# Routing groups of one and three batches in layer 0, norms batch by batch, and the next attention's first scores between the last up and down projections

## The chip, the cores and the metric

The kernel runs on one core of a Trainium2 chip. The metric is device time of one launch in microseconds. Three runs of the kernel before took 1347.03, 1354.06 and 1354.34 us; their median is 1354.06.

The engines are named as the profile names them: PE (TensorE: matmuls and transposes), DVE (VectorE), ACT (ScalarE), POOL (GpSimd) and SP (SyncE, which issues most of the transfers). Each engine executes one sequence of instructions; semaphores order them against each other.

## What is computed

Four layers, each an attention from 4 x 512 tokens (128 features) to 154 context tokens per batch, and then a mixture of 8 experts:

```python
x = x + L0_attention(layernorm(x), ctx)              # similarity features @ W_qv
x = x + L0_experts(layernorm(x))                     # top 2, (x W0 + b0) * silu(x W1 + b1), hidden 512
x = x + L1_attention(ctx, ctx, layernorm(x), mask)   # 16 heads of 8
x = x + L1_experts(layernorm(x))                     # top 1 with a capacity, gelu, hidden 512
x = x + L2_attention(layernorm(x), ctx)              # 16 heads of 64, its own norm, gated by tanh
x = x + L2_experts(layernorm(x))                     # top 2, gelu, hidden 256
x = x + L3_attention(layernorm(x), ctx, ctx)         # 16 heads of 64
x = x + L3_experts(layernorm(x))                     # top 2, relu, hidden 512
```

Layer 0's attention, for one batch:

```python
Sim  = (hc @ w1)[:, :, None] + (hq @ w2)[:, None, :] + einsum("bid,bjd->bij", hc * w3, hq) + b
A    = softmax(Sim, axis=2);  hq_hat = A @ hq
Batt = softmax(max(Sim, axis=2), axis=1);  hc_bar = Batt @ hc
out  = concat([hc, hq_hat, hc * hq_hat, hc * hc_bar]) @ W_qv + b_qv
```

The experts' part of the reference computes every expert for every token and weights the results; only the chosen one or two of each token count.

## The kernel before

**Tiles.** The tokens of a batch are four tiles of 128 rows (`NI` = 4), kept on chip as `x[b]` for the whole kernel. Attention works on one tile of a batch at a time in layers 1 to 3, and on a whole batch in layer 0.

**Routing.** The experts of a layer are computed in two halves, of batches 0 and 1 and of batches 2 and 3. `route` (L651) works on one half in steps with yields between: statistics, norm of both batches (L659), transposes (L251 in a helper), logits by the gate matrix, the best one or two experts (`top`), ranks of the tokens within their expert by matmuls with triangular and full matrices of ones (L693, L695), and from them a slot for each chosen pair of token and expert. The slots lie in blocks of 128, each block belonging to one expert. An indirect transfer on POOL (`scatter`, L721 and L722) writes 128 rows of the normed tokens to a DRAM buffer `buf[half]`; a half needs 16 of them with two choices and 8 with one. `BLK` gives the number of blocks, 23 with two choices (16 full ones at most, and 7 partly filled) or 15 with one.

**Experts.** `experts` (L825) is a generator too. SP loads tokens in groups of four blocks (`load`), which waits for all scatters of the half; PE transposes them (`tokens`, L850). For each block (or two, `PER`) `up` (L855) reads the expert's number, SP loads its weights, 516 KB in layer 0, into one of three buffers, and PE multiplies (L877); `down` (L882) of the block before applies the activation, multiplies by `w2` (L916), which holds all experts' down weights, copies the result on DVE and stores it to `ybuf[half]`. So a down always follows the next block's up.

**Gathering back.** `gather` (L948) queues indirect loads on POOL (L953) which bring each token's rows back; `row_transfers` (L641) takes the next `n` of the queued row transfers, scatters and gathers alike, and ties each to an instruction beside which it is to start. `combine` (L965) adds a token tile's gathered rows, weighted, to `x` (L971, DVE). A gather waits for all stores of the half; a `combine` of the first half was written behind the issue of all the half's gathers.

**Order.** `Steps` wraps a generator so that the main loop can interleave it with others by hand. The main loop (L1356 on) for a layer: the attention, with the combines of the last layer's second half and the routing of this layer's first half stepped beside it; the first experts, with the second half's routing; then the second experts, with the first half's gathers and combines and the preparation of the next attention (`at.early`: keys, values or masks; `at.late`: norm, transposes, queries). In the attentions of layers 2 and 3 PE, ACT and DVE keep the order as written (`wide_period`), in that of layer 1 PE and ACT do (`narrow_period`); elsewhere, layer 0's attention among it, a scheduler chooses each engine's order from its own estimate of times. Layer 0's attention (`attend_first`, L1278) prepares batches 0 to 3 (similarity and exponentials) and then finishes each in `tile_of` (L1026): transposes of the probabilities (L1033, L1038), their product with the context (L1041, L1042), the maxima over the tokens (L1048, L1051), `hcp` (L1060) and the output product.

Of the kernel before, what the change touches and what calls it, by code (L numbers as in the profile page):

```python
# [19 lines left out]
P = 128  # L20
# [6 lines left out]
E = 8  # L27
H = 16
CAP = int(B * S / E * 1.25) + 1
NH = NT // 2  # L30
EPS = 1e-5
NEG = -1e20
BLK = (2 * NH + E - 1, NH + E - 1)
UPS = (2, 1, 1, 1)
NF = (4, 4, 2, 4)
PER = (1, 2, 2, 2)


# [9 lines left out]
def tile_xattn_moe_stack(ctx: ExitStack, tc: tile.TileContext, a: dict, out: bass.AP):  # L48
# [101 lines left out]
    for base, sign in ((0, 1), (D // H - 1, -1)):  # L150
# [17 lines left out]
    fill = const.tile([P, E, NH], F32, name="fill")  # L168
    nc.gpsimd.iota(
        fill, pattern=[[0, E], [P, NH]], base=0, channel_multiplier=0, allow_small_or_imprecise_dtypes=True  # L170
# [6 lines left out]
    nth = const.tile([1, BLK[0], E], F32, name="nth")  # L177
    nc.gpsimd.iota(
        nth, pattern=[[1, BLK[0]], [0, E]], base=0, channel_multiplier=0, allow_small_or_imprecise_dtypes=True
# [59 lines left out]
    def norm(src, found, pool=None):  # L239
        mv, rstd = found  # L240
        xn = (pool or xnp).tile([P, NI, D], F32, tag="xn", name="xn", bufs=3 if pool else 2)
        for i in range(NI):
            nc.vector.tensor_scalar(
                xn[:, i, :], src[:, i, :], mv[:, i, 0:1], rstd[:, i : i + 1], ALU.subtract, ALU.mult
            )
        return xn
# [23 lines left out]
    class Tile:  # L270
# [31 lines left out]
        def exp(self, g):  # L302
            if g == 0:
                self.pr = p2.tile([P, H, S2], F32, tag="probs", name="probs")
            for s in range(min(3, 8 - 3 * g)):
                for j in range(2):
                    h = self.at.heads(None, 3 * g + s, j)
                    nc.scalar.activation(  # L308
# [5 lines left out]
                    )  # L314

# [44 lines left out]
        def take_ends(self, engine):  # L360
            self.tails = p2.tile([self.rows, 4, P], F32, tag="tails", name="tails")
# [124 lines left out]
    def wide_period(new, old, nxt=None, middle=nothing, queries=nothing, parts=nothing, after=nothing, older=None):  # L486

        if new:
            new.score(0)
# [3 lines left out]
        if new:  # L493
            new.most(0)
# [41 lines left out]
    def attention64(b, gather_x, wq, wk, wv, wo, add):  # L536
# [36 lines left out]
        def values_ends():  # L573
# [3 lines left out]
            for r in range(2):  # L577
                rows = slice(64 * r, 64 * r + 64)
                nc.tensor.matmul(q[rows, :], ct2[:, b], wv[:, r * 512 : (r + 1) * 512], start=True, stop=True)
# [6 lines left out]
            at.vt = at.vt.rearrange("p c s d -> p (c s d)")  # L586

# [35 lines left out]
    def rsm(name, *shape, dt=F32):  # L623
        return rt.tile([P, *shape], dt, tag=name, name=name)

    def top(lg):

        m = rt.tile([P, NH], F32, tag="m", name="m", bufs=4)
        nc.vector.tensor_reduce(m, lg, AX.X, ALU.max)
        eq = rt.tile([P, NH, E], F32, tag="eq", name="eq", bufs=4)  # L630
        nc.vector.tensor_tensor(eq, lg, bc(m, 2, E), ALU.is_equal)
        nc.vector.tensor_tensor(eq, eq, bc(rev_e, 1, NH), ALU.mult)
        r = rt.tile([P, NH], F32, tag="r", name="r", bufs=4)
        nc.vector.tensor_reduce(r, eq, AX.X, ALU.max)
        oh = rt.tile([P, NH, E], F32, tag="oh", name="oh", bufs=4)
# [5 lines left out]
    def row_transfers(n=2 * NH, behind=None):  # L641
# [9 lines left out]
    def route(layer, half, wg, bg, b2):  # L651

        lg = rsm("lg", NH, E)
        found = [stats(x[2 * half + k]) for k in range(B // 2)]
        yield
        xns = [norm(x[2 * half + k], found[k], rt) for k in range(B // 2)]  # L659
        yield  # L660
        xnTs = [transposed(xn) for xn in xns]
        yield
        for k, xnT in enumerate(xnTs):
            q = ps_tr()
            for i in range(NI):
                nc.tensor.matmul(q[:, i * E : (i + 1) * E], xnT[:, i * P : (i + 1) * P], wg, start=True, stop=True)
            o = lg[:, k * NI : (k + 1) * NI, :]
            qv = q[:, 0 : NI * E].rearrange("p (i e) -> p i e", i=NI)
            if bg is None:
                nc.vector.tensor_copy(o, qv)  # L670
            else:
                nc.vector.tensor_tensor(o, qv, bc(bg, 1, NI), ALU.add)
        yield
# [3 lines left out]
        sel = rsm("sel", NH + 1, E, dt=BF16)  # L677
        nc.vector.memset(sel[:, NH, :], 0.0)
        if layer == 1:
            nc.vector.tensor_copy(sel[:, 0:NH, :], oh1)  # L680
        else:
            yield
            lg2 = rsm("lg2", NH, E)
# [3 lines left out]
            nc.vector.tensor_tensor(sel[:, 0:NH, :], oh1, oh2, ALU.add)  # L687
# [3 lines left out]
        n = (NH + 1) * E  # L691
        q = ps_tr()
        nc.tensor.matmul(q[:, 0:n], before, sf, start=True, stop=False)  # L693
        for s in range(1, NH + 1):
            nc.tensor.matmul(q[:, s * E : n], ones_b, sf[:, 0 : n - s * E], start=False, stop=(s == NH))  # L695
# [737 lines left out]
```

## Time and profile before

| Quantity | Value |
|---|---|
| Median of three runs | 1354.06 us |
| The profiled execution | 1282.47 us |
| Its span | 1280.8 us |
| Mean granted PE clock | 0.917 of full speed |
| First expert matmul of layer 0 | 108.3 us |
| Layer 0's experts, 46 blocks | 108.3 to 260.5 us |
| Layer 1's attention | 259 to about 499 us |
| Layer 1's experts, to the end of the stage | about 481 to 574 us |
| Layer 2's attention | 571 to 817 us |
| Layer 3's attention | 904 to 1152 us |
| Last PE work | about 1251 us |

The profile is of one execution, and its times below are counted from the start of the span. The profiled execution was shorter than the median of the timed runs, so a difference read in the profile is to be set against 1282.47 us and then scaled.

Two rows of groups give the indirect transfers, of 128 rows each, which POOL issues (columns: line, engine, operation, what is written from what, count; busy time in all, mean ns of one; idle time of the engine just before, and what ended most of it):

```profile
L953 POOL DMA_INDIRECT yg<-ybuf,su x112 | 106.7, 952 | 246.5 <-ACT pT L267 59.9
L722 POOL DMA_INDIRECT buf<-xn,su x112 | 109.6, 979 | 227.0 <-DVE eb L745 97.3
```

### The profile page before, as it was taken

To read this page: it belongs to the slowest core of one execution; us is meant where nothing else is said; L and a number is where in the kernel's file an instruction comes from. 1 tells how busy PE (TensorE), PEld (TensorE's weight loads), DVE (VectorE), ACT (ScalarE), POOL (GpSimd) and SP (SyncE) were. 2 spreads that over 40 slices of the span, in tenths; PEclk is the share of its full clock that TensorE was granted. 3 is DMA by queue.
4 is the path that set the end of the run, shared out by engine and by line. 5 is a ranking of instruction groups with operands and counts; after the bars stand their busy time and mean duration, and the time that the engine had idled before them with its cause. 6 is when DMAs were issued, how large, how long until landed. Compare 5 with 4: busy or idle time off the path is not lost.

```text
span 1280.8 us, 26318 instructions
## 1 busy us (share of the span) xinstructions
PE 1089.4 (85%) x9351; PEld 896.9 (70%) x9351; DVE 731.6 (57%) x2012; ACT 565.3 (44%) x2264; POOL 253.6 (20%) x281
## 2 busy tenths in 40 slices
PE   4787998977878888889999998966899999899990
PEld 3657998933435448787878777855778788789890
DVE  6554646567666763335665776424476576646352
ACT  2113433454554543546656565321656665532230
POOL 2041315023000010232000004045220000402334
PEclk8767999988898988998999999887999999999996
DMA  7023786721100314433112214444421111334762
GB/s 228 1 81 113 216 253 189 207 94 25 23 19 26 100 38 119 133 110 84 35 35 55 64 37 123 123 150 133 127 55 45 41 35 35 109 95 143 209 191 60
DMA packets 136064, 126.77 MB, mean 99 GB/s; under 512 B 12538, under 2 KB 115583, under 8 KB 135551
## 3 DMA queue, kind: packets, MB, share of 16 engines
q1 hardware_dynamic: 128767, 110.39, 30.5%
q0 software_dynamic: 7168, 14.69, 3.9%
q8 instruction: 77, 1.26, 0.4%
q14 instruction: 52, 0.43, 0.1%
HBM read 101.31 MB, written 23.72 MB: 98 GB/s over the span
## 4 chain that ended last, share of the span: by engine, by line
PE 59%; DVE 12%; DMA 9%; issue 8%; ACT 5%; POOL 5%; SPq 2%; POOLq 0%; DVEq 0%
PE sc L877 11%; PE av L916 6%; PE tr L371 6%; PE sc L607 5%; PE av L408 5%; PE tr L425 5%; PE sc L592 3%; DMA yg<-ybuf,su 3%; POOL yg L953 3%; ACT probs L308 3%; DVE nm L294 3%; PE sc L1175 2%; DMA w<-in_up 2%; PE av L390 2%; PE tr L358 2%
## 5 line engine op out<-in xcount | busy, mean ns | idle before, releaser
L308 ACT ACTIVATE probs<-sc,nm 128x154 f32<-128x154 f32 x768 | 286.9, 403 | 162.7 <-DVE nm L294 162.5
L877 PE MATMUL sc<-tokT,w 128*128 128x128 f32 x1528 | 201.3, 286 | 8.7 <-DMA w<-in_up 3.6
L877 PEld LDWEIGHTS sc<-tokT,w 128*128 128x128 f32 x1528 | 189.0, 200 | 15.5 <-ACT eg L900 5.2
L294 DVE TENSOR_REDUCE nm<-sc 128x6 f32<-128x924 f32 x144 | 142.6, 1007 | 74.8 <-PE sc L607 49.1
L308 ACT ACTIVATION_READ_ACCUMULATOR probs<-sc,nm 128x1 f32 x768 | 168.3, 219 | 0.0
L916 PE MATMUL av<-w,hT 128*128 x1160 | 155.3, 279 | 3.2 <-DVE hT L905 2.5
L953 POOL DMA_INDIRECT yg<-ybuf,su x112 | 106.7, 952 | 246.5 <-ACT pT L267 59.9
L722 POOL DMA_INDIRECT buf<-xn,su x112 | 109.6, 979 | 227.0 <-DVE eb L745 97.3
L916 PEld LDWEIGHTS av<-w,hT 128*128 128x128 f32 x1160 | 141.9, 193 | 8.9 <-issue 4.7
L236 POOL TENSOR_TENSOR rstd<-ve,nhalf 128x4 f32<-128x4 f32 x32 | 33.0, 1032 | 547.3 <-DVE ve L234 429.6
L264 DVE COPY pT<-tr 128x512 f32<-128x512 f32 x160 | 106.9, 684 | 45.3 <-PE tr L371 41.5
L408 PE MATMUL av<-pT,vm 128*64 128x128 f32 (+1 forms) x1536 | 106.2, 284 | 22.5 <-DVE pT L264 22.4
L371 PE MATMUL tr<-ident,probs 128*128 128x128 f32 x768 | 123.1, 291 | 1.5 <-DVE rT L337 1.5
L371 PEld LDWEIGHTS tr<-ident,probs 128*128 128x128 f32 x768 | 86.1, 146 | 33.4 <-issue 21.7
L408 PEld LDWEIGHTS av<-pT,vm 128*64 128x64 f32 (+1 forms) x1536 | 63.8, 126 | 55.7 <-DVE pT L264 30.9
L900 ACT ACTIVATE eg<-sc,w 128x128 f32<-128x128 f32 x184 | 52.9, 368 | 89.5 <-PE sc L877 82.1
L607 PE MATMUL sc<-kT,qT 64*128 64x154 f32 x1024 | 87.1, 308 | 4.8 <-ACT probs L308 4.8
L905 DVE SCALAR_TENSOR_TENSOR hT<-sc,w,eg 128x128 f32<-128x128 f32 x184 | 56.2, 342 | 51.0 <-ACT eg L900 51.0
L607 PEld LDWEIGHTS sc<-kT,qT 64*128 64x128 f32 x1024 | 71.3, 189 | 15.8 <-issue 9.9
L592 PE MATMUL sc<-xnT,wq 128*128 128x128 f32 x512 | 73.6, 303 | 4.7 <-ACT probs L308 2.3
L592 PEld LDWEIGHTS sc<-xnT,wq 128*128 128x128 f32 x512 | 67.3, 212 | 10.2 <-issue 3.6
L425 PE MATMUL tr<-wo,aT 128*128 128x128 f32 x512 | 66.2, 284 | 1.6 <-DVE xnT L256 1.3
(255 smaller groups left out, 1432.2 us busy)
## 6 DMA issues: line engine op xcount, KB each, us to landing
w<-in_up SPq DMA_DIRECT2D x46, 516.0 KB
w<-in_up SPq DMA_DIRECT2D x76, 258.0 KB
rep<-rd SPq DMA_DIRECT2D x64, 256.0 KB
tok<-buf SPq DMA_DIRECT2D x36, 256.0 KB
ybuf<-ys SPq DMA_DIRECT2D x58, 128.0 KB
w<-in_down SPq DMA_DIRECT2D x3, 2048.0 KB
w<-in_up SPq DMA_DIRECT2D x46, 128.0 KB
ybuf<-ys SPq DMA_DIRECT2D x52, 64.0 KB
```

The source lines that it names most:

```text
L264: return nc.vector.tensor_copy(o, i)
L294: nc.vector.tensor_reduce(self.at.heads(self.nm, g, n), self.sc[g][:, :, 0 : n * S2].rearrange("p j (s k) -> p j s k", s=n), AX.X, ALU.max ...
L308: nc.scalar.activation(self.pr[:, h, :], self.sc[g][:, j, s * S2 : (s + 1) * S2], AF.Exp, bias=self.nm[:, h : h + 1], accum_out=self.rs[:, ...
L371: nc.tensor.transpose(q[:, t * P : (t + 1) * P], self.pr[:, h, 0:P], ident)
L408: nc.tensor.matmul(av[rows, cols], v, self.pT[n][:, t, :], start=False, stop=last)
L425: nc.tensor.matmul(o[:, 0:D], self.aT[:, c, :], self.at.wo[:, c, :], start=(c == 0), stop=(c == self.nb - 1))
L592: nc.tensor.matmul(sc[:, c // 4, c % 4 * P : (c % 4 + 1) * P], wq[:, c * P : (c + 1) * P], at.xnT[:, i * P : (i + 1) * P], start=True, sto ...
L607: nc.tensor.matmul(sc[:, j, s * S2 : (s + 1) * S2], at.qT[i][rows, c, :], at.kT[rows, c, :], start=True, stop=True)
L722: ins = nc.gpsimd.indirect_dma_start(out=buf[half], out_offset=bass.IndirectOffsetOnAxis(ap=su[:, t : t + 1], axis=0), in_=xns[t // NI][:, ...
L877: nc.tensor.matmul(dst, w[:, b, at : at + P], xT, start=True, stop=True)
L916: nc.tensor.matmul(y[:, b * D : (b + 1) * D], hT[:, fc, :], w2[:, bass.ds(es[b], 1), fc, :].rearrange("p o d -> p (o d)"), start=(fc == 0) ...
L953: ins = nc.gpsimd.indirect_dma_start(out=yg[:, t, :], out_offset=None, in_=ybuf[half], in_offset=bass.IndirectOffsetOnAxis(ap=su[:, t : t ...
```

## The change

- **Groups.** The halves become groups of batches by layer, `GROUPS`: in layer 0 the first group is batch 0 alone and the second is batches 1 to 3; in the other layers they stay as they were. Layer 0 then has 15 blocks in the first group and 31 in the second. Tiles, buffers and loops follow (`nt` in place of `NH`).
- **Single norms.** In layer 0, and for the second group everywhere, `route` takes statistics, norm, transposes and logits one batch at a time. The second group's route begins within the attention: in layer 0 beside `attend_first`, in the others after tile 1 of batch 3.
- **Layer 0's attention** gets its PE order as written; `tile_of` becomes a generator with a yield in its middle, and the product with the context moves behind the transpose of the maxima.
- **Gathers** are kept for each batch apart (`Gathered`). The first group's first `NI * TOP` gathers are issued at once, others with the downs (2 + n each instead of 2 n) or, for a `combine` that needs them, just ahead of it.
- **Layer 1.** Its setup moves behind the first experts of layer 0; its parts for each next batch are distributed over the tiles anew; and the exponentials of its first tile release three row transfers for each group of heads.
- **Token transposes** of the second group stand behind the early parts of the next attention (`ahead`).
- **First scores.** After the last block's up projections, and before its down projections, the next attention's first group of scores and its maximum are written; the first period then leaves them out.
- **Buffers.** Several routing tiles and `tails` get one buffer in place of two or four, the normed tiles of the routing four in place of three, and `yg` six of half the size in place of two.

```diff
+GROUPS = (((0,), (1, 2, 3)), ((0, 1), (2, 3)), ((0, 1), (2, 3)), ((0, 1), (2, 3)))
+TOP = (2, 1, 2, 2)
+def most_blocks(layer, half):
+    return TOP[layer] * NI * len(GROUPS[layer][half]) + E - 1
...
-        found = [stats(x[2 * half + k]) for k in range(B // 2)]
-        yield
-        xns = [norm(x[2 * half + k], found[k], rt) for k in range(B // 2)]
-        yield
-        xnTs = [transposed(xn) for xn in xns]
-        yield
+        for some in ([b] for b in batches) if layer == 0 or half else (batches,):
+            found = [stats(x[b]) for b in some]
+            if layer:
+                yield
+            new = [norm(x[b], f, rt) for b, f in zip(some, found)]
+            if layer:
+                yield
+            xnTs = [transposed(xn) for xn in new]
...
             for c in range(m):
-                nc.tensor.transpose(q[:, c * P : (c + 1) * P], tok[:, c, :], ident)
+                ins = nc.tensor.transpose(q[:, c * P : (c + 1) * P], tok[:, c, :], ident)
+                if g == 0:
+                    wait_for(ins, ahead, "they fill the wait for the tokens")
...
-                2 * n, nc.vector.tensor_copy(ys[:, 0:n], y[:, 0 : n * D].rearrange("p (b d) -> p b d", b=n))
+                2 + n, nc.vector.tensor_copy(ys[:, 0:n], y[:, 0 : n * D].rearrange("p (b d) -> p b d", b=n))
...
+        while got[k].begun < NI * len(routed[1]):
+            row_transfers(1)
+        for (cw, _), yg in zip(routed[1], got[k].rows):
+            nc.vector.scalar_tensor_tensor(xi, yg[:, i, :], cw[:, t : t + 1], xi, ALU.mult, ALU.add)
...
+        first, second = (Steps(route(layer, half, *gates[layer])) for half in range(2))
+        with tc.manual_schedule(engines={mybir.EngineType.PE}):
+            tiles = [prepare(b, found[b]) for b in range(2)]
+            tiles[0].step()
+            tiles[0].finish()
+            tiles.append(prepare(2, found[2]))
+            tiles[1].step()
+            first.step()
+            tiles[1].finish()
+            first.step(2)
+            tiles.append(prepare(3, found[3]))
+            first.step()
+            tiles[2].step()
+            first.step()
+            second.step()
+            tiles[2].finish()
+            first.step(2)
+            tiles[3].step()
+            second.step()
+            tiles[3].finish()
+            first.finish()
+        return first.result, second
...
+                    elif b == 3 and i == 1:
+                        first = beside.finish()
+                        beside = Steps(route(layer, 1, *gates[layer]))
...
-            at.parts = ((masks,), (xn, values), (xnT,), (keys_queries,))
+            at.parts = ((masks,), (values,), (xn,), (xnT, keys_queries))
...
-        second = Steps(route(layer, 1, *gates[layer]))
+        if layer:
+            second.step(4)
+            first.step(2 // PER[layer])
         while not second.done:
             second.step(2)
             first.step(2 // PER[layer])
         routed.append(second.result)
         stores = first.finish()
         row_transfers()
-        got = gather(0, routed[0], stores)
+        got = gather(layer, 0, routed[0], stores)
+        row_transfers(NI * TOP[layer])
+        early = ()
         if layer < 3:
+            if layer == 0:
+                prepare = setups[1]()
             at = prepare(0, found)
-            for part in at.early:
-                part()
-        second = Steps(experts(layer, 1, routed[1], w2)).step((9, 3, 5, 5)[layer])
+            early = [part() for part in at.early][-1:]
+        second = Steps(experts(layer, 1, routed[1], w2, early)).step((3, 2, 2, 2)[layer])
...
             at.queries(0)
+            second.step(-(-most_blocks(layer, 1) // PER[layer]) - second.taken)
+            at.tile = Tile(at, 0)
+            at.tile.score(0)
+            at.tile.most(0)
         stores = second.finish()
```

## The prediction

> **What bounds the kernel now.** I read the page's sums first. TensorE (PE) is busy 85% of the span and heads the chain that ended last, but that share is a mean over stages, so the row of 40 slices of 32 us, in tenths, says where it is not full.
>
> ```profile
> span 1280.8 us, 26318 instructions
> PE 1089.4 (85%) x9351; PEld 896.9 (70%) x9351; DVE 731.6 (57%) x2012; ACT 565.3 (44%) x2264; POOL 253.6 (20%) x281
> PE   4787998977878888889999998966899999899990
> PE 59%; DVE 12%; DMA 9%; issue 8%; ACT 5%; POOL 5%; SPq 2%; POOLq 0%; DVEq 0%
> ```
>
> The low digits stand at slices 0 to 3 (layer 0's attention), 8 to 10 (start of layer 1's attention), 26 and 27 (layer 2 to layer 3) and the end. The first and third are what the change can reach most directly; there I asked what PE waited for (columns: instruction, releaser, us in total, times, longest). From 0 to 110 us, then from 800 to 920 us:
>
> ```profile
> PE tr L251 <- DVE xn L243: 7.9, 2, 4.4
> PE tr L850 <- DMA tok<-buf: 6.5, 1, 6.5
> ...
> PE tr L693 <- DVE sel L687: 5.5, 1, 5.5
> ```
> ```profile
> PE tr L850 <- DMA tok<-buf: 11.0, 2, 10.1
> PE tr L251 <- DVE xn L243: 11.0, 2, 10.2
> ```
>
> L850 is the first transpose of an expert stage: it waits until the last scattered row has landed and the token block is read back. The timeline (start, length, instruction, in brackets the idle time before it and its releaser) shows why the routing blocks layer 0's attention: batch 2's `sim` is ready at 47 us, its transposes run at 69, because PE's sequence has the rank matmuls of the first half (L693) ahead of them.
>
> ```profile
> 47.01 0.79 DVE L1029 TENSOR_TENSOR sim<-sim,srinv 128x616 f32<-128x616 f32 x1
> ...
> 68.67 0.24 PE L693 MATMUL tr<-sel,before 128*128 128x72 bf16 x1 [5.48 <-DVE sel L687]
> ...
> 69.03 1.09 PE L1033 MATMUL tr<-ident,sim 128*128 128x128 f32 x4
> ```
>
> Between layers 2 and 3, 16 scatters fill POOL, PE waits for tokens, then the gathers come late and the next norm is late with them:
>
> ```profile
> 834.85 1.02 POOL L722 DMA_INDIRECT buf<-xn,su  x1 [14.98 <-DVE eb L745]
> ...
> 854.07 0.96 POOL L722 DMA_INDIRECT buf<-xn,su  x1 [0.30 <-issue]
> ...
> 859.38 1.97 PE L850 MATMUL tr<-ident,tok 128*128 128x128 f32 x8 [10.14 <-DMA tok<-buf]
> ...
> 867.16 0.98 POOL L953 DMA_INDIRECT yg<-ybuf,su  x1 [12.12 <-DVE ys L925]
> ```
>
> **What the skill says.** The Trainium skill, "TensorE: Matmul & The Clock Gate", section "Part 1: The HAM clock gate (the 'warmup' mystery)": PE's clock drops after an idle stretch and needs some us of work to return. The trace agrees: 0.62 granted in 64 to 96 us and 0.76 in 864 to 896, against 0.97 over layer 0's experts. The same page, section "The mechanism": matmuls start and end in program order, so one that waits holds all behind it; the L693/L1033 lines agree. "DMA: Bandwidth & Descriptors", section "Anatomy of one DMA — SWDGE (gpsimd) path": about 2 us fixed per transfer, mostly the confirmation. Here scatters land 2.3 us after issue and gathers 2.3 to 3.8, while POOL issues one every 1.27 us (0.96 and 0.30 idle), so for a series the pace decides. Same page, section "Issuing engines are not separate DMA queues": all transfers share the 16 engines; agrees, as layer 0's last `ybuf` store takes 7.12 us behind the 2 MB `in_down` load.
>
> **The change part by part**, summed against the profiled execution (1282.5 us, span 1280.8).
>
> *Layer 0, start of the experts.* They start at 108.3 us. After, the first group is batch 0 alone: 8 scatters (8 x 1.27 = 10 us) in place of 16, issued during later batches. The written order keeps the rank matmuls off the other batches' path. The three waits named above sum to 7.9 + 6.5 + 5.5 = 20 us; some of the norm's waits are early loads and stay. Worked the other way: layer 0's attention runs from about 12 to 98 us, some 64 of them with PE busy at a mean clock of 0.71; four batches at about 15.7 us each in an undisturbed rhythm, plus a tail, end at 88 to 91. I take a start at 90: **-18** (-14 to -24).
>
> *Layer 0, between the groups.* This is the price. The first group lasts 15 blocks, not 23. A block takes 152.2 / 46 = 3.3 us with its side work, so it ends at 90 + 50 = 140. The second group needs batch 3, then the ranks (over 12 tiles), slots and 24 scatters. Before, the second half's first scatter was issued at 140.15, 32 us after its experts began, behind both batches' norms; with batches 1 and 2 already done I take 28 us: 118.5. Then 24 x 1.27 = 30.5 gives 149; landing 2.3, the token read behind the weights on SP, some 3: 155. PE idles from 140 to 155, less some 2 us of layer 1's early keys and values, which the change puts ahead of the token transposes: **+13** (0 to +18). SP's queue also holds the next weight loads behind the token read; these 516 KB loads came at about 200 GB/s, 2.5 us each, inside the upper bound. The trace shows no token wait between 108 and 260 before, so this wait is new.
>
> *Layer 0, side work.* Batch 2's norm, transposes and logits leave the experts for the attention, about 3 us of PE at most: **-3**. Total blocks are 46 both times, hence no change in expert work. Moving layer 1's setup behind the first experts' start is paid nowhere: the ups cover it, in bounds ±1. Together layer 0 gives **-8** (0 to -18).
>
> *Layer 1's attention.* Before, 16 second-half gathers run from 274 to 300 us; VectorE's combines wait for them, 59 us in 58 waits over the run, and tile 3 of that stretch takes 20.8 us against 11 to 14 of its neighbours. After, there are 24 rows: 8 x 1.27 = 10 us more on POOL, three batches' worth of combines spread over more periods. VectorE runs in order, so a late combine holds the copies behind it (`pT`, for which PE waits). The exps release three rows each early on, which hides most: **+3** (0 to +9; up to +25 in the rival below).
>
> *Layer 1 to 2.* Gathers of the first batch go first, single norms spread the second route: **-2** (-4 to +2).
>
> *Layer 2 to 3.* The first batch's 8 gathers stand right behind the scatters, and its combine waits for these alone. `xn` was there at 888.8; 8 gathers from about 858 (8 x 1.27, landing 3) and the combines and norm give 871 to 874. The 10.2 us wait shrinks to about 3: **-7** (-5 to -11). The token wait of 10.1 stays, since its 16 scatters stay and only the second route is begun earlier; were it to vanish, a further -8.
>
> *Layer 3's second half* has earlier combines: **-1**. The end does not move: from 1251 us on PE is idle, 16 gathers and the last stores remain.
>
> *Scores and maximum between the last up and down projections.* The kernel before already runs them there, since the scheduler placed them so:
>
> ```profile
> 571.47 0.80 PE L607 MATMUL sc<-kT,qT 64*128 64x154 f32 x8
> 572.19 0.94 PE L916 MATMUL av<-w,hT 128*128 x6
> 573.06 0.53 PE L607 MATMUL sc<-kT,qT 64*128 64x154 f32 x2
> 573.93 1.31 PE L607 MATMUL sc<-kT,qT 64*128 64x154 f32 x14
> 574.50 2.15 DVE L294 TENSOR_REDUCE nm<-sc 128x6 f32<-128x924 f32 x2 [0.17 <-PE sc L607]
> ```
>
> Two of three score groups lie around the downs; what is left is one maximum of about 1 us per start: **-1** (0 to -3 over three layers).
>
> *Buffers* falling from 4 or 2 to 1 (`eq`, `t5`, `tails` and the like) are free while their users are in order on VectorE; `tails` (pt) with one buffer couples neighbouring batches: 0 to +3, taken as 0.
>
> Sum: -8 + 3 - 2 - 7 - 1 - 1 = **-16** us. The median of the runs, 1354.06, is 1354.06 / 1282.5 = 1.056 of the profiled execution; scaled, -17: **1337 us**. About 1% (13.5 us) is what can be told from no change.
>
> **Rivals.**
> *Given back in layer 0 and 1.* The second group's tokens come after 165 us instead of 155, since 24 scatters in a row cannot begin earlier; the wait then passes 18 us and with it goes the whole gain of layer 0, leaving -7 - 1 - 2 + 3, some -7 or less: 1347 (1341 to 1360). For it: scatters before began 32 us after the experts. Against: two of three batches are routed before. Chance 0.28.
> *Slower.* At layer 1's start the rows behind the first nine are issued only as the combines ask for them. VectorE is in order, so each pair costs a landing, about 3.5 us, before the next pair can be asked for: 6 or 7 such pairs on the copies' path make +20 to +26 in place of +3. If layer 0 gives less than 10 us, the sum is over zero: 1366 (1360 to 1378). For it: 59 us of combine waits are there already. Against: the exps issue rows ahead. It decides once tile periods beside the gathers pass 20 us for more than one tile. Chance 0.17.
> *Larger gain.* The second group's early route hides its wait, the 10.1 us before layer 3 go as well: -35 to -45, 1313 (1300 to 1322). Chance 0.12.
> *The named part does nothing* is what I assume already; it changes the attribution, 1 us, not the time.
>
> **The numbers.** Main case (1322 to 1346, at 1337) 0.43. Faster by over 1%, below 1340.5: 0.12 + about 0.37 of the main case + 0.03 = 0.52; slower: 0.17 + 0.01 = 0.18; within 1%: 0.30. The range 1308 to 1366 leaves out the lower end of the large gain and the upper half of the slower case.
>
> **What would show it.** Right: first expert matmul near 90; a new token wait at L850's successor around 140 to 155; xn wait before layer 3 about 3 us; downs at the same places. Wrong: layer 0's attention not shorter than 86 us, no token wait between the groups, or tile periods over 20 us in layer 1.

## The result and the profile after

The changed kernel is slower by 1.2%: median 1364.31 us (1358.43 to 1371.0, 9 runs) against 1347.70 (1341.67 to 1354.34, 9 runs) for the kernel before, ratio 1.0118 [1.0085, 1.0152]. (A ratio is a kernel's time over that of the kernel before, measured beside it, with its 95% interval.) The forecast was 1337 us, with a range of 1308 to 1366 and a chance of 0.18 for slower by over 1%.

The runs were made on several chips, and the kernel before takes about 1278 us on chip 4 and 1344 to 1350 us on chips 0, 7 and 8, so times are compared only with runs of the kernel before on the same chip. For the first trace of the kernel before (1282.47 us) and for the trace of the changed kernel (1368.49) no chip is on record, but the first agrees with chip 4 and the second with the others; their difference of 86 us is not what the change costs, and the factor of 1.056 by which the forecast scaled its sum is one between chips. The page of the changed kernel, with the rows shown of before:

```profile
span 1366.8 us, 26291 instructions
PE 1117.8 (82%) x9351; PEld 914.1 (67%) x9351; DVE 732.2 (54%) x2012; ACT 563.9 (41%) x2264; POOL 253.6 (19%) x281
PE   5779599957778788988999987948889999798881
PE 58%; DVE 14%; issue 8%; DMA 6%; ACT 5%; another core or an unknown queue 3%; POOL 3%; SPq 2%; POOLq 0%; DVEq 0%; ACTq 0%
```

PE, VectorE, ScalarE and POOL execute as many instructions as before. A slice is 34 us here. The low digits are where they were, with a new one at slice 4 (137 to 171 us), between layer 0's groups of experts, and a lower one at slice 8, the start of layer 1's attention. PE's waits there, from 135 to 180 us and from 268 to 330 us:

```profile
PE av L945 <- DVE hT L934: 6.7, 2, 6.4
PE tr L877 <- DMA tok<-buf: 4.4, 1, 4.4
PE sc L906 <- DVE tokT L98: 3.4, 1, 3.4
PE sc L906 <- issue: 2.4, 5, 1.2
```
```profile
PE av L419 <- DVE pT L273: 12.5, 3, 5.2
PE tr L382 <- DVE rT L348: 7.1, 1, 7.1
PE tr L369 <- DVE res L1234: 4.0, 2, 3.2
```

The first is the forecast wait between the groups, 17 us in four pieces. In the trace of `no_named` (below; 130 to 180 us), from chip 4, it is a single wait for the tokens:

```profile
PE tr L875 <- DMA tok<-buf: 12.0, 1, 12.0
```

The second is VectorE's: copies that PE needs come late. In the kernel before (`before_again`, 261 to 325 us) the same two waits were:

```profile
PE av L408 <- DVE pT L264: 6.7, 4, 2.9
PE tr L371 <- DVE rT L337: 0.8, 1, 0.8
```

The new first scores stand where the change puts them (timeline of the changed kernel: last up, the downs with the scores in between):

```profile
606.20 1.06 PE L906 MATMUL sc<-tokT,w 128*128 128x128 f32 x8
607.10 1.95 PE L945 MATMUL av<-w,hT 128*128 x16
608.98 1.06 PE L621 MATMUL sc<-kT,qT 64*128 64x154 f32 x12
609.96 1.16 PE L945 MATMUL av<-w,hT 128*128 x8
```

Four traces come from chip 4 and can be set side by side. `no_named` is the changed kernel without the first scores; it takes the same time as the changed one (below). Stages in us, from starts and ends in the timelines ("up" and "down" are an expert's two projections; `late_route` and `no_exp_rows` are experiments below, each the changed kernel with one part taken back):

| Stage | before, again | no_named | late_route | no_exp_rows |
|---|---|---|---|---|
| start to layer 0's first up | 109.0 | 96.2 | 98.3 | 98.5 |
| layer 0's experts, to the last down | 152.6 | 157.6 | 160.1 | 160.6 |
| layer 1's attention, to the next up | 220.6 | 235.4 | 233.9 | 220.4 |
| layer 1's experts | 95.6 | 99.4 | 91.7 | 94.7 |
| layer 2's attention | 232.4 | 231.8 | 229.1 | 230.1 |
| layer 2's experts | 98.9 | 92.0 | 90.5 | 90.1 |
| layer 3's attention | 236.0 | 237.2 | 236.4 | 237.2 |
| layer 3's experts | 106.8 | 111.6 | 110.2 | 110.8 |
| from the last down to the end | 28.5 | 28.3 | 28.7 | 28.2 |
| span | 1280.4 | 1289.7 | 1278.9 | 1270.7 |

Layer 0's start gains, though less than forecast, and layer 2's experts gain as forecast. Layer 1's attention takes 15 us more, layer 1's and layer 3's experts 4 and 5. A stage that no edit touches differs by up to 5 us between these traces (layer 0's last down: 253.9, 258.5, 259.1), so one difference of this size is not read by itself, only where several runs repeat it. The spans of the first two columns differ by 9 us, the medians of their timed runs by 15 (1278.35 and 1293.59): the table doesn't place all of the loss.

A *period* below is the time from the reciprocal of one attention tile (`rinv` on VectorE) to that of the next tile.

### The profile page after: what moved, and what is told of

It is laid out like the page before. It is cut to its first block, busy times and chain, and to the rows that moved or that the text cites. A ratio compares the mean times of both kernels' runs of the same rounds, so it can differ in the third digit from the quotient of the medians.

```text
span 1366.8 us, 26291 instructions
## 1 busy us (share of the span) xinstructions
PE 1117.8 (82%) x9351; PEld 914.1 (67%) x9351; DVE 732.2 (54%) x2012; ACT 563.9 (41%) x2264; POOL 253.6 (19%) x281
## 4 chain that ended last, share of the span: by engine, by line
PE 58%; DVE 14%; issue 8%; DMA 6%; ACT 5%; another core or an unknown queue 3%; POOL 3%; SPq 2%; POOLq 0%; DVEq 0%; ACTq 0%
PE sc L906 11%; PE av L945 8%; PE tr L382 6%; PE av L419 5%; PE sc L621 5%; PE tr L436 4%; ACT probs L317 2%; PE sc L1220 2%; DVE nm L303 2%; PE sc L606 2%; PE av L401 2%; POOL yg L990 2%; PE tr L369 2%; DVE pT L273 1%
## 5 line engine op out<-in xcount | busy, mean ns | idle before, releaser
L906 PE MATMUL sc<-tokT,w 128*128 128x128 f32 x1528 | 210.9, 290 | 27.8 <-issue 19.1
L906 PEld LDWEIGHTS sc<-tokT,w 128*128 128x128 f32 x1528 | 195.0, 204 | 36.2 <-issue 27.4
L945 PE MATMUL av<-w,hT 128*128 x1160 | 160.9, 287 | 26.3 <-ACT hT L915 10.6
L945 PEld LDWEIGHTS av<-w,hT 128*128 128x128 f32 x1160 | 147.3, 200 | 34.6 <-issue 13.1
L382 PE MATMUL tr<-ident,probs 128*128 128x128 f32 x768 | 124.4, 294 | 7.9 <-DVE rT L348 7.9
L382 PEld LDWEIGHTS tr<-ident,probs 128*128 128x128 f32 x768 | 87.4, 147 | 39.8 <-issue 23.0
L954 DVE COPY ys<-av 128x256 f32<-128x256 f32 (+1 forms) x110 | 39.1, 357 | 85.7 <-PE av L945 57.0
L436 PE MATMUL tr<-wo,aT 128*128 128x128 f32 x512 | 72.2, 301 | 2.6 <-DVE xnT L265 1.3
L436 PEld LDWEIGHTS tr<-wo,aT 128*128 128x128 f32 x512 | 68.2, 214 | 4.7 <-DVE xnT L265 1.9
```

What stands on the lines that cost most here:

```text
L382: nc.tensor.transpose(q[:, t * P : (t + 1) * P], self.pr[:, h, 0:P], ident)
L436: nc.tensor.matmul(o[:, 0:D], self.aT[:, c, :], self.at.wo[:, c, :], start=(c == 0), stop=(c == self.nb - 1))
L906: nc.tensor.matmul(dst, w[:, b, at : at + P], xT, start=True, stop=True)
L945: nc.tensor.matmul(y[:, b * D : (b + 1) * D], hT[:, fc, :], w2[:, bass.ds(es[b], 1), fc, :].rearrange("p o d -> p (o d)"), start=(fc == 0) ...
```

## The experiments

**The kernel before, again.**

> The kernel before, unchanged, to have a profiled execution that lies near its timed ones: the first one's span was 1281 us where nine timed runs lay between 1342 and 1354. If that execution was an exception, this span is near 1347 and some stages are longer than in the first trace, without the change; if profiled executions of this kernel are always short, it is again near 1281.

Measured: 1280.57 against 1278.35, ratio 1.0009 [0.9982, 1.0036], span 1280.4, on chip 4. Here timed and profiled executions agree, so a profiled execution of this kernel is not short as such. That the timed runs shown with the first profile came from another chip is inferred from this and from the times on chips 0, 7 and 8.

**Without the first scores (`no_named`).**

```diff
-            second.step(-(-most_blocks(layer, 1) // PER[layer]) - second.taken)
-            at.tile = Tile(at, 0)
-            at.tile.score(0)
-            at.tile.most(0)
...
-            new = at.tile
+            new = Tile(at, 0)
```

> The changed kernel without its last part: the next attention's first scores and maximum are no longer written between the last block's up and down projections, but at the start of the attention, as before. The forecast's theory (that part does nothing, since the order before had scores there already): within 3 us of the changed kernel, 1361 to 1367, ratio to before about 1.012. Rival (the written place holds up the last downs, their stores and so the gathers behind them): 8 to 16 us less than the changed kernel, a ratio of 1.000 to 1.006.

Measured: ratio 1.0127 [1.0083, 1.0172], against 1.0118 and (in `after_again`, below) 1.0126 with the first scores. The first scores do nothing that can be measured.

**Even groups in layer 0.**

```diff
-GROUPS = (((0,), (1, 2, 3)), ((0, 1), (2, 3)), ((0, 1), (2, 3)), ((0, 1), (2, 3)))
+GROUPS = (((0, 1), (2, 3)), ((0, 1), (2, 3)), ((0, 1), (2, 3)), ((0, 1), (2, 3)))
```

(The steps of the first route in `attend_first` follow.)

> The changed kernel with layer 0's groups of two and two batches again (23 and 23 blocks, 16 and 16 scatters), all else as changed. If the long series of 24 scatters and 24 gathers gives back the gain of the early start and costs layer 1's attention its periods (the forecast's slower rival), this is 10 to 25 us below the changed kernel, a ratio to before of 0.993 to 1.004. If the regrouping is a gain as forecast, it is 5 to 15 us above the changed kernel, a ratio of 1.016 to 1.023.

Measured: ratio 1.0130 [1.0090, 1.0169]. Neither: layer 0's last down ends at 272.5 us against 253.9 in `no_named`, layer 1's attention takes 224.5 against 235.4 and its experts 93.8 against 99.4. What groups of one and three gain in layer 0 is lost again behind it. The gain is not the regrouping's alone: the order written for PE in layer 0 was made for groups of one and three, while even groups in the scheduler's order end layer 0's experts at 261.6 in the kernel before and at 255.5 in `mixed_no_exp_rows` below.

**The second routes behind the attention (`late_route`).**

```diff
-        for some in ([b] for b in batches) if layer == 0 or half else (batches,):
+        for some in ([b] for b in batches) if layer == 0 else (batches,):
...
-                    elif b == 3 and i == 1:
-                        first = beside.finish()
-                        beside = Steps(route(layer, 1, *gates[layer]))
...
-        return first, beside, old, older
+        return beside.finish(), Steps(route(layer, 1, *gates[layer])), old, older
...
-        if layer:
-            second.step(4)
-            first.step(2 // PER[layer])
```

> The changed kernel with the second group's route in layers 1 to 3 put behind the attention again and its norms, transposes and logits taken for both batches together, as before; layer 0 as changed. If the route beside the last attention tiles lengthens those tiles (the waits on reciprocals and transposes at tiles 14 and 15 of layers 2 and 3), this is 8 to 15 us below the changed kernel; if it saves work behind the attention as forecast (2 us at layer 1, 1 at layer 3), it is 2 to 8 us above it.

Measured: ratio 0.9990 [0.9964, 1.0017], against 1.0127 for `no_named` on the same chip. The early beginning with its single norms, booked in the forecast as a small saving, costs 1.4%: by itself as much as the whole loss. Of the difference of 11 us between the two traces, 8 lie in layer 1's experts. The last two tiles, which the expectation suspected, are not longer: layer 1's last two periods take 17.4 and 11.4 us in both. Three further runs tell which part of the change it is:

> The changed kernel with the second group's route in layers 1 to 3 begun behind the attention, but batch by batch as changed (the late-route run took both batches together). If the early beginning is what costs, this equals the late-route run: ratio to before 0.996 to 1.003. If taking the norms singly is what costs (eight steps of waits in place of four between the first blocks), it stays at the changed kernel: 1.008 to 1.016.

Measured for `late_single`: ratio 1.0024 [1.0001, 1.0047]: it is the early beginning (1.0% against `after_again`, the changed kernel on the same chip), not the single norms, though these may cost 0.3%.

> The changed kernel with the first group's route in layers 1 to 3 finished after tile 1 of batch 3, as changed, but nothing routed beside the last two tiles; the second route behind the attention with both batches together. If it is the forced finish (the first route's last steps in one go, in order on VectorE) that holds up the last tiles, this stays near the changed kernel, 1.008 to 1.016; if it is batch 2's norm, transposes and logits beside the last two tiles, it equals the late-route run, 0.996 to 1.003.

Measured for `early_finish`: ratio 1.0017 [0.9998, 1.0036]: not the forced finish of the first route, but what follows from routing batch 2 beside the last tiles.

> The changed kernel with the late route, both batches together, in layer 1 alone; layers 2 and 3 route early as changed. If the cost lies in layer 1 (its experts were 8 us longer with the early route), this gains most of the 15 us: ratio 0.998 to 1.006. If it is spread evenly over the three layers, a third of it: 1.006 to 1.011.

Measured for `late_in_1`: ratio 1.0070 [1.0045, 1.0096]. The value is in the range of an even spread, its interval reaches into the other: layer 1 has something like half of the cost.

The changed kernel was run beside these three, for its trace.

> The changed kernel, unchanged, for a trace that stands beside those of the other runs. All theories: ratio to before 1.008 to 1.016. The theory formed from the first runs (the early second route in layers 1 to 3 costs some 15 us, most of it from the first block of layer 1's experts on) expects layer 1's experts to last some 99 us from the first up to the last down, against 92 with the late route and 96 in the kernel before, and layer 1's attention some 227 us from the last down of layer 0 to its last score, against 215 before.

Measured: ratio 1.0126 [1.0068, 1.0184]. Layer 1's experts take 97.8 us, against 91.1 in `late_single`, 90.1 in `late_in_1` and 94.9 in `early_finish` (whose traced execution was 8 us longer than its median). Its attention takes 241 to 242 us in all four; the 227 expected came from traces of chip 4. PE in layer 1's experts, changed kernel (first fence) and `late_single` (second fence), from the attention's last projection (L436) to the ranks (L717):

```profile
528.59 0.39 PE L436 MATMUL tr<-woT,aT 128*128 128x128 f32 x2
532.11 1.24 PE L260 MATMUL tr<-ident,xn 128*128 128x128 f32 x4 [3.14 <-DVE xn L252]
534.03 1.88 PE L689 MATMUL tr<-wg,xnT 128*128 128x8 f32 x8 [0.68 <-ACT xnT L102]
537.74 0.24 PE L717 MATMUL tr<-sel,before 128*128 128x72 bf16 x1 [1.83 <-DVE sel L704]
...
539.98 4.17 PE L906 MATMUL sc<-tokT,w 128*128 128x128 f32 x22 [0.78 <-DVE tokT L98]
```
```profile
524.17 0.39 PE L436 MATMUL tr<-woT,aT 128*128 128x128 f32 x2
524.40 0.60 PE L260 MATMUL tr<-ident,xn 128*128 128x128 f32 x4
...
528.74 2.50 PE L906 MATMUL sc<-tokT,w 128*128 128x128 f32 x20
...
531.29 1.50 PE L906 MATMUL sc<-tokT,w 128*128 128x128 f32 x12
...
538.94 0.20 PE L717 MATMUL tr<-sel,before 128*128 128x72 bf16 x1
```

With batch 2 done early, PE has only batch 3's chain left: it waits at each link (3.14, 0.68, 1.83 us), and from 527.0 to 540.0 us no up projection runs. With batch 2 left for later, its transposes and two blocks' ups fill the same stretch, and the gap between ups is 6 us. The ranks come 28 us after the first up in the changed kernel and 32 in `late_single`: the early work brought the ranks 4 us forward, and PE waited 5.7 us on the way to them.

**The early route, its last steps interleaved with blocks.**

```diff
-        if layer:
-            second.step(4)
-            first.step(2 // PER[layer])
```

> The changed kernel with the early route kept, but the second route's last four steps (batch 3's statistics, norm, transposes, logits) no longer written in one piece ahead of the next block: two steps, a block, two steps, a block. Theory: with batch 2 done early nothing is left beside batch 3's chain, and PE's order puts its transposes (waits of 3.1 and 1.8 us in layer 1) ahead of ready up projections; if the piece is at fault, layer 1's experts shrink from some 98 us (slower chip) to 91 to 94 and the ratio falls to 1.004 to 1.010. Rival (the order comes from the missing work of batch 2, not from the piece, or the cost lies in the attention's last tiles): layer 1's experts stay at 97 or more, ratio 1.010 to 1.015.

Measured: ratio 1.0065 [1.0044, 1.0087], layer 1's experts 89.0 us. As expected, with experts that are shorter still; with the early route kept, the place of four steps is worth about 0.6% (against 1.0126 on another chip, with intervals that overlap), and PE's wait for batch 3's norm falls to 1.36 us:

```profile
534.67 1.95 PE L945 MATMUL av<-w,hT 128*128 x16
537.97 1.10 PE L260 MATMUL tr<-ident,xn 128*128 128x128 f32 x4 [1.36 <-DVE xn L252]
```

**Layer 1's combines from tile 2 on (`even_step2`),** on top of even groups.

```diff
-                    step = nothing if (b, i) in ((0, 0), (2, 0)) or layer > 1 and (b, i) == (0, 1) else beside.step
+                    step = nothing if (b, i) in ((0, 0), (0, 1), (2, 0)) else beside.step
```

> The run with even groups (ratio 1.013) with one edit more: in layer 1's attention the combines of the last layer's second group begin at tile 2, as before the change, not at tile 1. Theory: VectorE's order puts combines that wait for gathers ahead of tile 1's copies, so the period from tile 0 to tile 1 is 21.3 us in place of 13.4; with the edit it is back at 13 to 15 and the ratio is 1.005 to 1.009. Rival (that period is long because the exponentials of the first tile release the gathers, whatever the combines do): it stays above 18 us, ratio 1.011 to 1.015.

Measured: ratio 1.0189 [1.0150, 1.0229], first period 23.9 us. The theory fell; the rival, right on the period though the ratio lies above its range too, named the release of gathers by the first tile's exponentials, which was tried next.

**No release by the exponentials (`no_exp_rows`),** in the changed kernel otherwise untouched.

```diff
-            if self.at.dh < 64 and self.at.first and self.i == 0:
-                row_transfers(3, ins)
```

> The changed kernel with one edit: the exponentials of layer 1's first tile no longer release three gathers each. Theory formed from the run even_step2, whose own theory fell: the early release makes the scheduler place combines ahead of the maximum and the copy of the reciprocals in VectorE's order, and these combines then wait for gathers that cannot start before the last store has landed, so the first period is 21 to 25 us. Without it: first period 13 to 17 us and a ratio of 1.004 to 1.009. Rival (24 gathers have to be waited for somewhere; the later they start, the longer the second and third periods): the sum of the first three periods stays at 60 us or more, ratio 1.010 to 1.018.

Measured: ratio 0.9937 [0.9913, 0.9962], first three periods 11.3 + 14.9 + 17.5 = 44 us, against 59 in `no_named` and 48 in the kernel before (all on chip 4). Two lines turn a loss of 1.2% into a gain of 0.6%, more than the theory gave. The start of layer 1's attention, `no_named` (first fence) and this run (second fence); L1012 are combines, `nm` is a maximum of the scores, `rT` is the copy that the transposes of probabilities (L382, in the second fence L380) wait for:

```profile
262.48 1.00 POOL L988 DMA_INDIRECT yg<-ybuf,su  x1 [92.89 <-DMA ybuf<-ys]
...
265.06 0.35 DVE L1012 SCALAR_TENSOR_TENSOR x<-yg,wa,x 128x128 f32<-128x128 f32 x1 [3.53 <-DMA yg<-ybuf,su]
266.40 0.35 DVE L1012 SCALAR_TENSOR_TENSOR x<-yg,wb,x 128x128 f32<-128x128 f32 x1 [0.98 <-DMA yg<-ybuf,su]
...
267.84 1.11 DVE L303 TENSOR_REDUCE nm<-sc 128x6 f32<-128x924 f32 x1
...
269.18 0.27 DVE L348 COPY rT<-tr 16x128 f32<-16x128 f32 x1
269.51 1.11 PE L382 MATMUL tr<-ident,probs 128*128 128x128 f32 x4 [7.02 <-DVE rT L348]
```
```profile
267.07 1.12 DVE L303 TENSOR_REDUCE nm<-sc 128x6 f32<-128x924 f32 x1 [0.36 <-PE sc L1218]
268.11 0.27 DVE L346 COPY rT<-tr 16x128 f32<-16x128 f32 x1
268.43 0.66 PE L380 MATMUL tr<-ident,probs 128*128 128x128 f32 x4 [0.77 <-DVE rT L346]
...
270.09 1.00 POOL L988 DMA_INDIRECT yg<-ybuf,su  x1 [98.26 <-DVE pT L273]
...
273.30 0.35 DVE L1012 SCALAR_TENSOR_TENSOR x<-yg,wa,x 128x128 f32<-128x128 f32 x1 [1.74 <-DMA yg<-ybuf,su]
```

In the first, the gathers are let go with the exponentials but start only when the last store (`ybuf<-ys`) has landed; the combines stand ahead of the maximum and of `rT` in VectorE's order and wait for rows, and PE waits 7 us behind them. In the second, gathers start behind a `pT` copy, 11 us after the last down in place of 8.6, and the combines stand behind the copies. Starting the gathers later made the attention shorter. That the order follows from an estimate of the scheduler in which released gathers arrive at once is inferred; the order itself is in the trace.

**What gained, put together (`mixed`):** even groups, layer 0's attention in the scheduler's order, late second routes, combines from tile 2, and the early gathers and short steps in layers 1 and 2 only (of the edit, only the last part is shown; `...` marks what is left out):

```diff
-                2 + n, nc.vector.tensor_copy(ys...
+                2 * n if layer in (0, 3) else 2 + n, nc.vector.tensor_copy(ys...
...
-        row_transfers(NI * TOP[layer])
+        row_transfers(NI * TOP[layer] if layer in (1, 2) else 0)
...
-        second = ....step((3, 2, 2, 2)[layer])
+        second = ....step((9, 2, 2, 5)[layer])
```

> Of the changed kernel, only what the traces showed to gain: gathers by batch with early combines in layers 1 and 2, the moved setup and layer 1's parts, the first scores; layer 0 with even groups, its attention in the scheduler's order and late combines; the second routes behind the attention; layer 3 with late gathers as before. Expected by stage against the kernel before: layers 0's stages 0, layer 1's attention -2 to +2, layer 1's experts -4, layer 2's attention -3, layer 2's experts -8, layer 3 0: ratio 0.985 to 0.995. If the early gathers gained only because layer 0's regrouping moved other work, 0.997 to 1.003.

Measured: ratio 0.9846 [0.9794, 0.9898], at the lower end of the expectation; layer 1's first period stays at 24.0 us. The kernel before has no trace from this chip, so the stages can't be set against it. Without the release by the exponentials:

> The mixed kernel (ratio 0.985), likewise without the release by the exponentials; its layer 0 has even groups, so 16 gathers come into layer 1's attention. Theory: first period 13 to 15 us in place of 24, ratio 0.978 to 0.983. Rival: the time is only moved into the following periods, as the kernel before shows them (13.4, 16.2, 18.6); ratio 0.983 to 0.988.

Measured: 0.9841 [0.9806, 0.9877], first period 12.4 us, span 1247.4. The value lies in the rival's range and the interval in both. This run is on chip 4, and by stage it gains where `mixed` was expected to: against the kernel before, layer 1's attention and experts take 8 and 6 us less, layer 2's 3.5 and 9 us less; layer 0's experts also begin 7 us earlier, which was not expected. Both again, on one chip:

> The mixed kernel again, beside the next one on the same chip, since the two were measured on different chips (0.985 and 0.984). If the release costs with even groups too, as its first period of 24 us says, this is 0.5 to 1% above the next one; if the time is only moved, they are within 0.3%.

> The mixed kernel without the release, again: 0.978 to 0.987. Against late_no_exp_rows of this call it tells what groups of one and three batches bring once nothing gives it back: 5 to 10 us for them by the earlier start of the experts (12 us, less the wait for the second group's tokens), 0 or less by the rival that the wait takes all.

Measured: `mixed` 0.9857 [0.9784, 0.9930], without the release 0.9792 [0.9723, 0.9861]. The first period shortens each time (24.2 to 12.2 us here, the first three from 53 to 45), but the intervals of the ratios overlap; for even groups the gain is not established. With layer 3's late gathers its experts take 106.1 us on chip 4, against 109 to 112 with the early ones, and 122 to 124 on chips 7 and 8, against 127 to 129 with the early ones on chips 0 and 7: these late gathers and combines go with the 3 to 5 us, though no run changed them alone.

**Groups of one and three, both costs removed.** This is `late_route` and `no_exp_rows` together, with layer 3's gathers late.

> The changed kernel with its groups of one and three batches in layer 0, and three edits: no release of gathers by the first exponentials (alone: 0.994), second routes of layers 1 to 3 behind the attention (alone: 0.999 against 1.012), gathers and combines of layer 3's first group as late as before (its experts were 5 us longer). If the two costs are independent, they add: 0.978 to 0.985, and the regrouping itself is worth what this lies below the even-group kernel of the same call. Rival (both edits remove the same loss, a late end of the first periods and routes): 0.988 to 0.995.

Measured: 0.9855 [0.9795, 0.9914], first three periods 48 us, layer 0's last down at 267.3, against 261.3 in `mixed_no_exp_repeat`. The value lies just above the upper end of the expectation, and its interval reaches into the rival's range too, so the times don't settle whether the two costs add. By stage both gains are there: layer 1's attention takes 216.1 us and its experts 89.0, against 241.3 and 97.8 in `after_again` (another chip). Against `mixed_no_exp_repeat` this kernel starts layer 0's experts 7 us earlier (97.0 against 104.4) and ends them 6 us later, and the medians lie 10 us apart, this one above; the gain of 5 to 10 us expected of the regrouping is not there, and a loss is not shown, since the intervals overlap. The two kernels also differ in the order of layer 0's attention and in the place of layer 0's gathers and combines, so neither sign is the regrouping's alone. On chip 4, too, layer 0's experts end at 255.5 with even groups (`mixed_no_exp_rows`) and at 253.9 to 259.1 in three kernels with groups of one and three: no gain of the regrouping by the end of layer 0 is shown. Its best form stays open.

## Why the prediction was wrong

The loss comes from two terms that the forecast booked as about nothing or as a gain, layer 1's attention and the early routes. Term by term:

- **Layer 0's start, -18:** -11 to -13 at the first up (109.0 to 96.2 and 98.5). The direction is right, the size outside the bounds of -14 to -24. The traces show 6.5 us of what is missing: PE's written order has batch 2's transposes ahead of batch 3's `hcp`, and the norm's `rstd` runs on POOL, behind the first group's eight scatters (`no_named`):

```profile
82.98 1.04 POOL L245 TENSOR_TENSOR rstd<-ve,nhalf 128x4 f32<-128x4 f32 x1
84.06 1.11 DVE L252 TENSOR_SCALAR xn<-x,mv,rstd 128x128 f32<-128x128 f32 x4 [4.80 <-POOL rstd L245]
84.55 1.15 PE L260 MATMUL tr<-ident,xn 128*128 128x128 f32 x4 [6.53 <-DVE xn L252]
```

- **Between the groups, +13, and layer 0 in all, -8:** the wait is 12.0 us in `no_named` and 17 in the changed kernel's trace, the tokens come at 159 us in `no_named`, between the 155 of the forecast and the 165 of its first rival, and layer 0's last down moves by -2.5 to -7.7. Right within its bounds.
- **Layer 1's attention, +3:** this is the first step that failed: "The exps release three rows each early on, which hides most". The release was counted as cover and was the cost: +15 us in the stage, 1.9% between the ratios with and without it (1.0127 in `no_named` and 0.9937, both on chip 4). The number of 24 gathers, which the step did price, costs little: without the release the first three periods take 44 us on chip 4, less than with 16 gathers before (48), and on chip 8 they take 48 with 24 gathers and 45 with 16.
- **Layers 1 to 2, -2, and "only the second route is begun earlier":** the second step that failed. Moving batch 2's norm, transposes and logits into the attention was booked as a saving of work behind it. It cost 1.4% over three layers, single norms included (1.0127 in `no_named`, 0.9990 in `late_route`). In layer 1's experts the traces show why: it took away what covered batch 3's chain, and the experts took 99.4 us in place of 91.7. For layers 2 and 3 this is not shown.
- **Layers 2 to 3, -7:** right. Layer 2's experts fall by 6.9 us, the longest wait for `xn` from 10.0 to 4.3 us on chip 4, and the token waits stay at about 10.
- **Layer 3's second half, -1:** +3 to +5. Early combines there have no attention behind them that profits; that they hold up the experts' work on VectorE is argued, and the kernels with late gathers don't have these 3 to 5 us.
- **First scores, -1:** nothing measurable, as the forecast's reason had it: the scheduler had placed them there already.

The slower rival had the mechanism half right, VectorE's order with combines in it, and its point of decision was met (two periods of 21 and 20 us). Its time, 1366 us (1360 to 1378), covers the measured 1364, but in part by luck: it had rows released too late, where they were released too early, and it put the whole price there, where the early routes cost about three quarters as much again.

## What to carry to other kernels

A transfer that is let go early does not start early if its source is not complete; what it moved here is its consumers' place in VectorE's order, and these then held back the copies that PE needs. Before work is moved out of a stage to shorten it, look for what that work was covering: a chain of small dependent steps needs ready work beside it, and the idle time appears where the cover was. And before two traces are compared, an untouched stretch with the same kind of work has to take the same time in both: here attention periods without row transfers agreed to 0.1 us on all chips, while one kernel took 5% longer on some chips than on another.

## What the runs showed of the hardware

One and the same kernel, the one before, took 1278 and 1277 us in two series of runs on chip 4, and 1347, 1350 and 1344 us on chips 0, 7 and 8. Four attention periods of layer 2 that have no row transfers beside them take 12.6, 15.5, 14.1 and 15.3 us on all four chips. Beside indirect transfers, in the traces of chips 0, 7 and 8 and in that of the changed kernel, PE issues single weight loads and matmuls at steps of 0.7 or 1.4 us with no releaser that the profile knows (changed kernel, layer 3's experts, gathers of POOL in between):

```profile
1299.53 0.37 PE L906 MATMUL sc<-tokT,w 128*128 128x128 f32 x1 [1.83 <-issue]
1299.73 0.95 POOL L990 DMA_INDIRECT yg<-ybuf,su  x1 [0.30 <-issue]
1300.93 0.37 PE L906 MATMUL sc<-tokT,w 128*128 128x128 f32 x1 [1.03 <-issue]
1300.98 0.94 POOL L990 DMA_INDIRECT yg<-ybuf,su  x1 [0.30 <-issue]
1302.33 0.37 PE L906 MATMUL sc<-tokT,w 128*128 128x128 f32 x1 [1.03 <-issue]
```

PE's matmuls of the experts waited 25 us without a known releaser in this trace (19.1 and 5.9 by the list of waits), 16 to 34 us in those of chips 0, 7 and 8, and at most 1.5 us in any trace of chip 4. This is at most half of the 70 us between the chips; where the rest lies and what differs between the chips is not known.
